# A two-layer graph network over 64 graphs: intermediate sums and scores in PSUM, byte masks, a third transposition tile, and new instruction orders

## The chip, the cores and the metric

The kernel runs on one core of one Trainium2 chip. Its engines work in parallel, each through its own queue in order: TensorE (PE) multiplies matrices into PSUM, which has eight banks of 128 partitions by 512 words of fp32; VectorE (DVE) and ScalarE (ACT) read and write PSUM and SBUF; GpSimd (POOL) works in SBUF alone; SyncE (SP) issues nearly all transfers here. PEld is TensorE's loading of weights. The metric is the device time of the whole program in microseconds (us).

## The reference

Input are 64 graphs of 256 nodes with 256 features each (`x`), with an adjacency `adj` of zeros and ones, and weights. Everything is fp32. Two layers follow each other; cut to what is computed:

```python
# layer 0
def gat(h, W, a):
    Wh = h @ W
    e = leaky_relu(Wh @ a[:F] + swap(Wh @ a[F:]), 0.2)
    att = softmax(where(adj > 0, e, -9e15), axis=1)
    return att @ Wh
h = layernorm(x + gat(gat(x, W1, a1), W2, a2)) * g + b          # norm A
x = layernorm(h + relu(h @ w_ff1 + b_ff1) @ w_ff2 + b_ff2)      # norm B, with g, b
# layer 1: 8 heads of 32
attn = softmax(q @ k.T / sqrt(32))
out = sum over r of (attn * (adj == r)) @ v_r                   # only r = 0 and 1 occur
x = layernorm(x + out @ Wo + bo)                                # norm C, with g, b
x = layernorm(x + gelu(x @ W1 + b1) @ W2 + b2)                  # norm D, with g, b
```

## The kernel before

A graph is small: 256 nodes are two tiles of 128 partitions, and the 256 features two blocks. Weights stay in SBUF. Most products over two by two blocks are made with seven instead of eight block products (`seven_products`: pieces `a` to `e` on TensorE, `k1` to `k4` that take a block out of PSUM, `p1` to `p3` that add to it).

One graph's work is cut into 194 **pieces**, each a function that issues a few instructions, named stage.piece. Each engine runs its instructions in the order in which the pieces are called, and nothing reorders them. Three lists set that order. `PERIOD` is one turn of the steady loop: an entry `G.gA0/0` calls piece `gA0` of stage G for the graph that is 0 behind the newest, `T.fd/5` a piece for the graph five behind. So six graphs are in flight. `START` and `END` are written-out lists for the first and last turns; setup pieces (S) stand in START. TensorE's steps in one turn, in the order of the list before: wh0, T.hd, wh1, ve, f1, eA, T.he, sc0, o0, o1, F.ha, F.hb, wo, F.hc, T.fa, T.fb, F.hd, gA0, gA1, T.fc, va, vb, eB, T.fd, F.he, vc, T.fe, q, k, T.ha, gB, T.hb, sc1, vd, T.hc, f0.

The pieces that the text speaks of:

- **L**: `xT`, `adj`, `x` load a graph. `joint_weights` (L338) makes the product `w12` of W1 and W2 and the four extra columns of `wx` once, ahead of the first graph.
- **G**, the two graph attentions (function `gat`, L732). `away` turns the adjacency into bytes that are 1 where there is no edge (L739) and takes its maximum (L742). `wh0`, `wh1` project; `wc` copies out. For step A: `eA` transposes one column into PSUM (L763), `lrA` on ACT writes the scores `s` to SBUF (L771), `adA` on DVE applies the leaky slope (L776), adds the mask (L777) and takes the maximum (L779), `exA` on ACT takes exponentials in place (L784), `rzA` divides the projected rows by their sums into `whz` (L791, L794), `gA0`, `gA1` multiply (L800), `wd` copies out. Step B is the same with `eB` to `rzB`, and ends in `gB`, tile `gat_b`.
- **Norms** (L493): `ln` adds the residual to the product in PSUM and writes `acc` in SBUF (L502), then takes statistics (L507 to L510); `rs` on POOL makes the factor (L514); `nm` normalises on DVE into `y` (L519). `ra`, `rb` on POOL scale and shift for the next residual.
- **Transpositions** (`turned`, L461): `dt` transposes 16-bit pairs by DMA into `pairs` (L469), `dm` moves halves by two transfers into `halves` (L477), and `c` (or `mg` for a head) joins them by a copy (L484), on ACT but for two heads that go to POOL. All these transfers are issued on SP in order. Eleven transpositions a graph share the tiles `pairs` and `halves`.
- **F**, the first feed-forward: `s` sums on POOL, `ha` to `he` with `hk`, `hp`, then `r` (ReLU), `f0`, `f1`; then `q`, `k` with their evictions `qe`, `ke`.
- **A**, the heads, two groups of four: `sc` scores, `mx` maxima (DVE), `ex` exponentials (ACT), `rz`, `sp` scaling (POOL), `dt`, `dm`, `mg` transposition, `pm` the mask (DVE, L922: the head's weights times the adjacency), `va` to `ve` the values, `o` outputs, `oc` evictions.
- **T**: `wo`, norm C, the second feed-forward (`ha` to `he`, GELU in `ge`, sums `u` on POOL, `fa` to `fe` with keeps `fk` on DVE at L713 and sums `fp`), norm D, `out`.

All PSUM tiles come from one tag of eight buffers, one bank each (`mm_tile`, L208).

Of the kernel before, what the change touches and what calls it, by code (L numbers as in the profile page):

```python
# [1312 lines left out]
```

## Time and profile before

| What | Value |
|---|---|
| Time, median of 3 runs | 3129.46 us (3119.91 to 3135.92) |
| The profiled execution: time, span | 3121.47 us, 3119.7 us |
| Mean granted TensorE clock | 0.992 |
| DMA moved | 449.41 MB, 144 GB/s |
| Heads' mask, L922 | 512 times, mean 1123 ns |
| Heads' transposition | 1024 transfers of halves (two for each of 512), 3.3 us to landing |

The page is of one profiled execution. A group's line gives the source line, engine, operation, output and inputs with shapes, count, then busy us, mean ns of one, and the engine's idle time just before it with what ended it. A busy PE includes the overlap of pipelined products, so its share says less than the spacing of like products does.

### The profile page before, as it was taken

How to read it: one execution, taken by the hardware profiler on the slowest of the kernel's cores; microseconds unless marked ns; L12 is line 12 of the kernel's file. 1: busy time of each engine (PE TensorE's matmuls, PEld its weight loads, DVE VectorE, ACT ScalarE, POOL GpSimd, SP SyncE). 2: the span in 40 equal slices, each digit the busy share in tenths (PEclk: the TensorE clock that was granted, in tenths of full speed). 3: DMA queues.
4: the chain of work that ended last, by engine and by line, in shares of the span. 5: the costliest groups of instructions: out<-in, count | busy, mean ns of one | idle time of the engine just before them, and what ended most of it. 6: DMA issues, size and time to landing. Idle time of an engine off the chain costs nothing.

```text
span 3119.7 us, 68789 instructions
## 1 busy us (share of the span) xinstructions
PE 3007.0 (96%) x23270; PEld 2629.7 (84%) x23270; DVE 2747.0 (88%) x5744; ACT 2548.7 (82%) x5822; POOL 2290.2 (73%) x3057
## 2 busy tenths in 40 slices
PE   6899999999999999999999999999999999999986
PEld 5788888888888888888898888888888888888876
DVE  5689999899998899898999899999999999889965
ACT  2688888888888888888888888888888888878874
POOL 4568777777777777777777777777777777777765
PEclk9999999999999999999999999999999999999998
DMA  5577766677676777776676666677677776767663
GB/s 156 108 145 149 149 149 143 146 155 143 149 151 137 142 146 151 148 152 138 155 150 144 148 142 145 150 152 147 147 153 145 149 149 143 146 138 151 149 133 73
DMA packets 1023941, 449.41 MB, mean 144 GB/s; under 512 B 771008, under 2 KB 1021888, under 8 KB 1023584
## 3 DMA queue, kind: packets, MB, share of 16 engines
q1 hardware_dynamic: 1022320, 442.70, 67.9%
q8 instruction: 188, 3.08, 0.5%
q0 software_dynamic: 976, 1.72, 0.4%
q14 instruction: 169, 1.38, 0.2%
q10 hardware_dynamic: 288, 0.52, 0.1%
HBM read 58.87 MB, written 16.78 MB: 24 GB/s over the span
## 4 chain that ended last, share of the span: by engine, by line
PE 68%; DVE 12%; DMA 8%; issue 3%; ACT 3%; POOL 1%; SPq 1%; DVEq 0%; ACTq 0%; POOLq 0%
PE ff_a L686 11%; PE hX_c L661 6%; PE o L930 5%; PE fX_c L702 5%; PE hX_a L661 4%; PE sc L880 3%; PE q L835 3%; PE hY_c L661 3%; PE k L835 3%; PE gat_b L800 3%; PE vX L848 3%; PE wh L747 3%; DVE pm L922 2%; PE wo L949 2%; DMA adj<-in_adjT 2%
## 5 line engine op out<-in xcount | busy, mean ns | idle before, releaser
L484 ACT COPY pm<-halves_p 128x1024 uint16<-128x1024 uint16 x384 | 522.4, 1360 | 137.8 <-DMA halves_p<-pairs_p 135.7
L922 DVE TENSOR_TENSOR pm<-pm,adj 128x512 f32<-128x512 f32 x512 | 565.6, 1123 | 19.3 <-POOL pm L484 12.2
L686 PE MATMUL ff_a<-w_L_gnn_w_ff,hid_a 128*128 128x256 f32 x2048 | 463.0, 379 | 0.1
L686 PEld LDWEIGHTS ff_a<-w_L_gnn_w_ff,hid_a 128*128 128x128 f32 x2048 | 384.0, 190 | 50.4 <-ACT hid_a L678 0.8
L484 POOL COPY pm<-halves_p 128x1024 uint16<-128x1024 uint16 x128 | 180.2, 1408 | 157.5 <-DMA halves_p<-pairs_p 140.4
L930 PE MATMUL o<-pm,v 128*32 128x256 f32 x4096 | 235.3, 381 | 5.5 <-POOL p L907 2.4
L678 ACT ACTIVATE hid_a<-hid_a,col_L_gnn_b_ff 128x256 f32<-128x256 f32 x512 | 230.1, 500 | 3.3 <-DVE hid_a L637 3.2
L678 ACT ACTIVATE hid_c<-hid_c,col_L_gnn_b 128x256 f32<-128x256 f32 x512 | 224.4, 498 | 5.1 <-DVE hid_c L637 2.4
L930 PEld LDWEIGHTS o<-pm,v 128*32 128x32 f32 x4096 | 126.2, 110 | 104.6 <-issue 15.9
L702 PE MATMUL fX_c<-f_L_gnn_W,hid_c 128*128 128x128 f32 x1536 | 207.2, 278 | 7.3 <-ACT hid_c L678 5.1
L514 POOL TENSOR_TENSOR rstd_a<-var_a,neghalf 128x2 f32<-128x2 f32 x64 | 45.0, 702 | 222.5 <-DVE var_a L510 222.5
L702 PEld LDWEIGHTS fX_c<-f_L_gnn_W,hid_c 128*128 128x128 f32 x1536 | 192.8, 192 | 13.2 <-ACT hid_c L678 5.8
L661 PEld LDWEIGHTS hX_a<-cols_a,f_L_gnn_w_ff 128*128 128x128 f32 x1024 | 126.9, 195 | 33.1 <-ACT hid_c L678 22.2
L880 PE MATMUL sc<-kT,qT 32*128 32x256 f32 x2048 | 149.6, 400 | 3.3 <-ACT p L894 2.8
L584 POOL TENSOR_TENSOR S_c<-cols_c 128x128 f32<-128x128 f32 x128 | 58.3, 455 | 128.4 <-ACT cols_c L484 128.4
L800 PE MATMUL gat_a<-whz_A,s_A 128*128 128x258 f32 x512 | 134.9, 400 | 18.2 <-DVE whz_A L794 15.4
L661 PE MATMUL hX_a<-cols_a,f_L_gnn_w_ff 128*128 128x128 f32 x1024 | 144.6, 285 | 6.4 <-ACT cols_a L484 5.0
L747 PE MATMUL wh<-wx,xT 128*128 128x260 f32 x512 | 136.0, 390 | 12.5 <-DVE wx L372 10.1
L661 PEld LDWEIGHTS hX_c<-S_c,f_L_gnn_W 128*128 128x128 f32 x1024 | 134.0, 191 | 8.5 <-ACT hid_c L672 1.3
L702 PE MATMUL fY_c<-f_L_gnn_W,H_c 128*128 128x128 f32 x1024 | 137.3, 278 | 3.8 <-POOL H_c L584 3.8
L661 PE MATMUL hX_c<-cols_c,f_L_gnn_W 128*128 128x128 f32 x1024 | 135.8, 276 | 2.7 <-ACT cols_c L484 2.7
L661 PE MATMUL hX_a<-S_a,f_L_gnn_w_ff 128*128 128x128 f32 x1024 | 136.9, 277 | 0.0
(2760 smaller groups left out, 9808.9 us busy)
## 6 DMA issues: line engine op xcount, KB each, us to landing
halves_p<-pairs_p SPq DMA_DIRECT2D x1024, 128.0 KB, 3.3
xT<-in_xT SPq DMA_DIRECT2D x64, 256.0 KB, 3.4
adj<-in_adjT SPq DMA_DIRECT2D x64, 256.0 KB, 3.5
x<-in_x SPq DMA_DIRECT2D x64, 256.0 KB, 3.5
halves_y_a<-pairs_y_a SPq DMA_DIRECT2D x128, 128.0 KB, 3.0
halves_y_y<-pairs_y_y SPq DMA_DIRECT2D x128, 128.0 KB, 3.5
halves_y_c<-pairs_y_c SPq DMA_DIRECT2D x128, 128.0 KB, 3.2
out<-res_d SPq DMA_DIRECT2D x64, 256.0 KB, 2.6
```

What stands on the lines that cost most here:

```text
L484: copy(into().bitcast(U16).rearrange("p (n s) -> p s n", s=2), t["halves"].rearrange("p s k q -> p s (k q)"),)
L661: nc.tensor.matmul(ps[:, f * P : (f + 1) * P], weights()[0][:, factor, f * P : (f + 1) * P], left, start=start and f == 0, stop=f == FC // ...
L678: nc.scalar.activation(tiles["hid"][:, f, :], tiles["hid"][:, f, :], func, bias=b1[:, f : f + 1])
L686: nc.tensor.matmul(tiles["ff"][:, i, :], tiles["hid"][:, f, nodes(i)], weights()[2][:, f, :], start=(f == 0), stop=(f == FC - 1),)
L702: nc.tensor.matmul(ps, left[:, f, :], weights()[2][:, factor, f * P : (f + 1) * P], start=start and f == 0, stop=f == FC // 2 - 1, skip_gr ...
L747: nc.tensor.matmul(t["whp", j], tiles["xT"][:, c, nodes(j)], wx[:, c, :], start=(c == 0), stop=(c == KC - 1),)
L800: nc.tensor.matmul(ps, t["s"][:, j, nodes(i)], t["whz"][:, j, :width], start=(j == 0), stop=(j == NT - 1),)
L835: nc.tensor.matmul(t[key + "p"][:, o, :], w[:, c, nodes(o)], tiles["cols"][:, c, :], start=(c == 0), stop=(c == KC - 1),)
L848: nc.tensor.matmul(ps, left, wv[:, factor, :], start=start, stop=True, skip_group_check=True)
L880: nc.tensor.matmul(t["sc", g, hh][:, i, :], qkv["q"][hd, g, nodes(i)], qkv["k"][hd, g, :], start=True, stop=True,)
L922: nc.vector.tensor_tensor(pm[:, 1, :], pm[:, 0, :], tiles["adj"], ALU.mult)
L930: nc.tensor.matmul(ps[hh * DH : (hh + 1) * DH, :], qkv["v"][:, j, d0 : d0 + DH], t["pm", (g, hh)][:, r, j * N : (j + 1) * N], start=(r == ...
```

## The change

- **Norms A, B and C:** the sum is written back into the product's PSUM tile; statistics and `nm` read it there, and the tile is let go after `nm`. The `acc` tiles in SBUF serve only norm D and setup.
- **First attention:** `e` takes a whole bank. The slope step reads `s` in SBUF and writes `e`, the mask step and the maximum work in `e`, and the exponentials read `e` and write `s`. One `s` tile instead of two.
- **Heads' mask:** `pm` compares the bytes of `away` with 0 and multiplies, instead of multiplying by the 32-bit adjacency. `away` has four tiles instead of one, `adj` one instead of four.
- **Tiles:** three each of `pairs`, `halves` and `S` instead of two.
- **Joint weights:** W1 is loaded on ACT's queue, its column products stand ahead of those of the joint product, and sums are written straight into `wx`.
- **Orders:** PERIOD, START and END are new. PERIOD has the same 194 pieces; 25 of them have another lag. TensorE's steps now: f0, T.hd, f1, wh0, T.he, wh1, sc0, o0, o1, T.fa, wo, eA, T.fb, F.ha, F.hb, T.fc, F.hc, va, T.fd, gA0, F.hd, gA1, T.fe, vb, F.he, eB, k, q, vc, T.ha, sc1, T.hb, vd, gB, ve, T.hc.

```diff
@@ -41,120 +41,121 @@
 PERIOD = """
-G.nmA/1 A.mx13/3 A.rz12/3 F.raB/4 F.sB/3 T.hk3/5 A.mx11/3 A.rz10/3 L.xT/0 T.hp3/5 A.vp2/4 A.dm02/4
-A.pm03/4 G.wh0/0 A.mg02/4 T.hd/5 A.ex13/3 T.hp2/5 G.wh1/0 A.ex11/3 A.sp12/3 A.dm00/4 G.wc0/0
-A.sp10/3 G.wc1/0 A.ve/4 A.pm01/4 F.dtA/1 A.mg00/4 F.dmA/1 F.f1/2 A.pm02/4 G.eA/0 A.pm00/4 T.rbC/5
-F.rbB/4 A.vk4/4 T.he/5 T.ge0/5 A.rz11/3 A.pm11/4 A.rz13/3 A.dt10/3 F.lnB/2 A.sc0/3 A.o0/4 T.ge1/5
-A.mx00/3 G.lrA/0 F.cA/1 T.hk4/5 A.o1/4 T.ge2/5 A.sp11/3 A.sp13/3 A.mx02/3 A.dt12/3 F.ha/1 A.oc0/4
-T.ge3/5 L.adj/0 A.oc1/4 F.sA/1 A.ex00/3 F.hb/1 A.mx03/3 G.away/0 A.dm10/3 A.dm12/3 F.rsB/2 F.hk1/1
-F.hk2/1 T.wo/4 A.mx01/3 G.adA/0 A.mg10/3 T.u0/5 F.hp1/1 T.lnC/4 F.hc/1 T.u1/5 A.mg12/3 A.dt13/3
-G.exA/0 F.raA/1 A.dt11/3 F.nmB/2 A.ex03/3 A.dm13/3 G.rzA/0 T.fa/5 F.hk3/1 A.ex02/3 T.rsC/4 T.fb/5
-F.hd/1 T.nmC/4 G.gA0/0 T.u3/5 T.fk1/5 T.fk2/5 A.rz03/3 A.ex01/3 T.u2/5 F.hp2/1 L.x/0 F.hp3/1
-A.mg13/3 A.sp03/3 G.gA1/0 A.pm12/3 G.wd0/0 G.wd1/0 A.dm11/3 A.rz01/3 T.fc/5 A.va/3 A.vb/3 F.dtB/2
-T.fk3/5 A.mg11/3 F.rbA/1 A.sp01/3 F.r0/1 A.pm13/3 T.dtC/4 A.rz02/3 A.vk1/3 G.eB/0 T.fd/5 F.dmB/2
-T.fp1/5 A.vk2/3 G.lrB/0 T.fp2/5 F.cB/2 F.he/1 A.vc/3 T.dmC/4 T.fe/5 A.rz00/3 F.r1/1 G.adB/0
-A.dt03/3 T.cC/4 A.dt01/3 F.q/2 A.vk3/3 G.exB/0 F.hk4/1 A.vp3/3 T.fp3/5 F.qe0/2 F.k/2 A.sp02/3
-T.fk4/5 F.r2/1 T.ha/4 F.qe1/2 A.dm03/3 F.ke0/2 T.hk1/4 T.lnD/5 G.rzB/0 T.nmD/5 A.sp00/3 T.sC/4
-G.gB/0 A.vp1/3 T.hb/4 A.dm01/3 T.rsD/5 A.dt02/3 T.raC/4 F.ke1/2 T.rbD/5 T.hp1/4 A.sc1/2 T.out/5
-A.dt00/3 G.lnA/0 A.mg03/3 T.hk2/4 F.r3/1 A.mg01/3 A.mx12/2 A.mx10/2 A.vd/3 G.rsA/0 T.hc/4 A.pm10/3
-F.f0/1 A.ex12/2 A.ex10/2
+T.hk3/5 A.ex12/3 F.f0/2 A.mx10/3 T.hd/5 A.pm00/4 G.rsA/1 A.vk4/4 L.xT/0 A.mg02/4 A.dm03/4 T.hp3/5
+F.f1/2 T.raC/5 A.ex10/3 G.nmA/1 T.hp2/5 A.pm02/4 A.mg03/4 A.rz12/3 G.wh0/0 T.he/5 T.ge0/5 L.adj/0
+A.pm01/4 T.ge1/5 G.wc0/0 A.sp13/3 A.dt11/3 F.dtA/1 A.pm03/4 T.rbC/5 F.lnB/2 A.sp12/3 A.dm11/3
+T.hk4/5 A.dt13/3 A.pm12/4 A.rz10/3 G.wh1/0 T.ge2/5 A.sc0/3 F.rsB/2 A.mx02/3 A.o0/4 F.dmA/1 T.ge3/5
+G.wc1/0 F.nmB/2 A.sp10/3 F.raA/1 A.o1/4 A.mx03/3 T.u0/5 A.mx01/3 T.fa/5 A.dt12/3 A.mx00/3 A.ex02/3
+A.dm13/3 L.x/0 A.oc0/4 A.oc1/4 F.cA/1 F.dtB/2 T.wo/4 A.dt10/3 G.away/0 G.eA/0 T.u1/5 T.u3/5
+A.ex03/3 A.ex01/3 G.lrA/0 F.sA/1 T.fk1/5 F.dmB/2 T.fp1/5 T.fb/5 A.mg11/3 F.ha/1 A.dm10/3 T.lnC/4
+F.hb/1 T.fk2/5 G.adA/0 A.rz03/3 A.rz01/3 T.fc/5 T.rsC/4 T.u2/5 F.hk1/1 F.hk2/1 A.sp01/3 T.nmC/4
+F.hc/1 T.fk3/5 F.hp1/1 A.ex00/3 G.exA/0 F.hk3/1 A.va/3 T.dtC/4 A.mg13/3 A.rz02/3 F.cB/2 G.rzA/0
+T.fp3/5 A.pm11/3 F.hp3/1 T.fd/5 A.sp02/3 G.gA0/0 F.hd/1 G.wd0/0 F.raB/3 T.fp2/5 A.mg10/3 A.rz00/3
+G.gA1/0 A.sp00/3 F.hp2/1 A.vk1/3 T.fe/5 T.fk4/5 A.vb/3 A.vk2/3 G.wd1/0 T.lnD/5 A.pm13/3 F.r0/1
+F.he/1 A.dt01/3 G.eB/0 F.k/2 F.q/2 A.vp1/3 F.r1/1 T.dmC/4 G.lrB/0 T.cC/4 A.dm12/3 G.adB/0 F.ke0/2
+F.hk4/1 F.ke1/2 A.vc/3 A.vk3/3 A.sp03/3 T.sC/4 A.dm01/3 T.ha/4 F.qe0/2 F.qe1/2 G.exB/0 A.dt00/3
+A.dt02/3 T.hk1/4 A.vp3/3 A.sc1/2 T.hb/4 A.vd/3 T.nmD/5 G.rzB/0 F.r2/1 T.hp1/4 A.mx11/2 A.mg01/3
+A.mx13/2 A.dt03/3 T.rsD/5 F.rbB/3 A.dm00/3 G.gB/0 T.hk2/4 A.vp2/3 A.pm10/3 T.rbD/5 A.mx12/2 F.r3/1
+A.ex11/2 F.rbA/1 A.mg12/3 A.rz11/2 A.dm02/3 G.lnA/0 A.ex13/2 F.sB/2 A.mg00/3 T.out/5 A.rz13/2
+A.ve/3 A.sp11/2 T.hc/4
 """.split()
...
@@ -322,7 +323,7 @@
             nc.sync.dma_start(out=tiles["xT"], in_=xT[b].rearrange("(c p) n -> p c n", p=P))
 
         def adjacency():
-            adj = tiles["adj"] = io.tile([P, NT * N], I32, tag="adj", name=f"adj_{b}", bufs=4)
+            adj = tiles["adj"] = io.tile([P, NT * N], I32, tag="adj", name=f"adj_{b}", bufs=1)
             nc.sync.dma_start(
                 out=adj.rearrange("p (t i) -> p t i", t=NT),
                 in_=adjT[b].rearrange("(t p) i -> p t i", p=P),
@@ -343,13 +344,15 @@
             work.tile([P, KC, D], F32, tag="y", name=f"in_{n}", bufs=3) for n in ("w1T", "w2", "w1")
         )
         a1, a2 = (work.tile([P, 2, D], F32, tag="acc", name=f"in_{n}", bufs=2) for n in ("a1", "a2"))
-        for a, n in ((a2, "L0_gnn_a2"), (a1, "L0_gnn_a1")):
+        for a, n in ((a1, "L0_gnn_a1"), (a2, "L0_gnn_a2")):
             nc.scalar.dma_start(
                 out=a.rearrange("p s d -> p (s d)"),
                 in_=t[n].rearrange("n one -> (n one)").partition_broadcast(P),
             )
-        for w, n in ((w1T, "L0_gnn_W1T"), (w2, "L0_gnn_W2"), (w1, "L0_gnn_W1")):
-            nc.sync.dma_start(out=w, in_=t[n].rearrange("(c p) n -> p c n", p=P))
+        for queue, w, n in (
+            (nc.sync, w1T, "L0_gnn_W1T"), (nc.scalar, w1, "L0_gnn_W1"), (nc.sync, w2, "L0_gnn_W2"),
+        ):
+            queue.dma_start(out=w, in_=t[n].rearrange("(c p) n -> p c n", p=P))
         for entry in ("L.xT", "L.adj", "L.x"):
             first.pop(entry)()
         ps = mm_tile("w12")
@@ -359,17 +362,14 @@
                     ps[:, o, :], w1T[:, c, nodes(o)], w2[:, c, :],
                     start=(c == 0), stop=(c == KC - 1),
                 )
-        nc.vector.tensor_copy(wx[:, :, :D], ps)
-        for w, a, at in ((wx, a2, SRC2), (w1, a1, SRC1)):
+        for w, a, at in ((w1, a1, SRC1), (wx, a2, SRC2)):
+            if w is wx:
+                nc.vector.tensor_copy(wx[:, :, :D], ps)
             for c in range(KC):
-                both = small.tile([P, 2], F32, tag="wa", name=f"wa_{at}_{c}", bufs=1)
                 prod = work.tile([P, 2, D], F32, tag="res", name=f"prod_{at}_{c}", bufs=3)
-                nc.vector.tensor_tensor(
-                    prod, a, w[:, c, :D].unsqueeze(1).to_broadcast([P, 2, D]), ALU.mult
-                )
-                nc.vector.tensor_reduce(both, prod, AX.X, ALU.add)
-                nc.vector.tensor_copy(wx[:, c, at : at + 1], both[:, 1:2])
-                nc.vector.tensor_copy(wx[:, c, at + 1 : at + 2], both[:, 0:1])
+                for half in range(2):
+                    nc.vector.tensor_tensor(prod[:, half, :], a[:, 1 - half, :], w[:, c, :D], ALU.mult)
+                nc.vector.tensor_reduce(wx[:, c, at : at + 2], prod, AX.X, ALU.add)
         return wx
 
 
@@ -465,14 +465,14 @@
         t = {}
 
         def turn():
-            t["pairs"] = work.tile([P, 2, 4, P], U16, tag="pairs", name=f"pairs_{name}", bufs=2)
+            t["pairs"] = work.tile([P, 2, 4, P], U16, tag="pairs", name=f"pairs_{name}", bufs=3)
             nc.sync.dma_start_transpose(
                 out=t["pairs"].rearrange("p c k q -> p (c k) q"),
                 in_=src().rearrange("p c a b n -> p (c a b n)").bitcast(U16),
             )
 
         def part():
-            t["halves"] = work.tile([P, 2, 4, P], U16, tag="halves", name=f"halves_{name}", bufs=2)
+            t["halves"] = work.tile([P, 2, 4, P], U16, tag="halves", name=f"halves_{name}", bufs=3)
             for c in range(2):
                 nc.sync.dma_start(
                     out=t["halves"][c * 64 : (c + 1) * 64].rearrange("p s k q -> p s (k q)"),
@@ -493,13 +493,13 @@
     def layernorm(do, stage, key, name, src, last=None):
 
 
+
         tiles = {}
 
         def sums():
-            acc, *terms = src()
-            if terms:
-                acc = work.tile([P, NT, D], F32, tag="acc", name=f"acc_{name}", bufs=2)
-                nc.vector.tensor_tensor(acc, *terms, ALU.add)
+            acc, *residual = src()
+            if residual:
+                nc.vector.tensor_tensor(acc, acc, *residual, ALU.add)
             tiles["acc"] = acc
             stats = small.tile([P, NT, 6], F32, tag="stats", name=f"stats_{name}", bufs=2)
             mv = tiles["mv"] = small.tile([P, NT, 2], F32, tag="mv", name=f"mv_{name}")
@@ -587,7 +587,7 @@
 
 
         def sums():
-            s = tiles["S"] = work.tile([P, 4, P], F32, tag="S", name=f"S_{name}", bufs=2)
+            s = tiles["S"] = work.tile([P, 4, P], F32, tag="S", name=f"S_{name}", bufs=3)
             cols = tiles["cols"]
             blocks = [cols[:, c, nodes(i)] for i in range(NT) for c in range(KC)]
             add_sums(nc.gpsimd, blocks, [s[:, n, :] for n in range(4)], range(4))
@@ -735,9 +735,9 @@
         t = {}
 
         def away():
-            t["away"] = work.tile([P, NT, N], U8, tag="away", name=f"away_{b}", bufs=1)
+            tiles["away"] = work.tile([P, NT * N], U8, tag="away", name=f"away_{b}", bufs=4)
             nc.vector.tensor_scalar(
-                t["away"].rearrange("p t i -> p (t i)"), tiles["adj"], 0.0, 1.0, ALU.is_le, ALU.mult
+                tiles["away"], tiles["adj"], 0.0, 1.0, ALU.is_le, ALU.mult
             )
             nc.vector.tensor_reduce(most[:, b : b + 1], tiles["adj"].bitcast(U32), AX.X, ALU.max)
 
@@ -758,31 +758,34 @@
 
         def targets(step, col):
 
-            ps = t["e"] = mm_tile(f"e_{step}{b}", (P, N))
+            t["e"] = mm_tile(f"e_{step}{b}", (P, NT, N))
             for i in range(NT):
                 nc.tensor.transpose(
-                    ps[:, nodes(i)],
+                    t["e"][:, 0, nodes(i)],
                     t["wh", step][:, i, col : col + 1].to_broadcast([P, P]), ident,
                 )
 
         def terms(step, col):
-            s = t["s"] = work.tile([P, NT, N], F32, tag="s", name=f"s_{step}{b}", bufs=2)
+            s = t["s"] = work.tile([P, NT, N], F32, tag="s", name=f"s_{step}{b}", bufs=1)
             for j in range(NT):
                 nc.scalar.activation(
-                    s[:, j, :], t["e"], AF.Identity, bias=t["wh", step][:, j, col : col + 1]
+                    s[:, j, :], t["e"][:, 0, :], AF.Identity,
+                    bias=t["wh", step][:, j, col : col + 1],
                 )
 
         def maximum(step):
-            nc.vector.scalar_tensor_tensor(t["s"], t["s"], ALPHA, t["s"], ALU.mult, ALU.max)
-            nc.vector.scalar_tensor_tensor(t["s"], t["away"], NEG, t["s"], ALU.mult, ALU.add)
+
+            nc.vector.scalar_tensor_tensor(t["e"], t["s"], ALPHA, t["s"], ALU.mult, ALU.max)
+            away = tiles["away"].rearrange("p (t i) -> p t i", t=NT)
+            nc.vector.scalar_tensor_tensor(t["e"], away, NEG, t["e"], ALU.mult, ALU.add)
             t["m"] = small.tile([P, NT], F32, tag="gm", name=f"gm_{step}{b}")
-            nc.vector.tensor_reduce(t["m"], t["s"], AX.X, ALU.max, negate=True)
+            nc.vector.tensor_reduce(t["m"], t["e"], AX.X, ALU.max, negate=True)
 
         def exps(step):
             t["z"] = small.tile([P, NT], F32, tag="gz", name=f"gz_{step}{b}")
             for j in range(NT):
                 nc.scalar.activation(
-                    t["s"][:, j, :], t["s"][:, j, :], AF.Exp,
+                    t["s"][:, j, :], t["e"][:, j, :], AF.Exp,
                     bias=t["m"][:, j : j + 1], accum_out=t["z"][:, j : j + 1],
                 )
 
@@ -821,7 +824,7 @@
             do[f"G.ad{step}"], do[f"G.ex{step}"] = partial(maximum, step), partial(exps, step)
             do[f"G.rz{step}"] = partial(over_sums, step, width)
         do["G.gB"] = second
-        return layernorm(do, "G", "A", f"a{b}", lambda: (None, t["gat"], tiles["x"]))
+        return layernorm(do, "G", "A", f"a{b}", lambda: (t["gat"], tiles["x"]))
 
     def projections(do, b, tiles):
 
@@ -919,7 +922,9 @@
         def by_relation(h):
 
             pm = t["pm", h]
-            nc.vector.tensor_tensor(pm[:, 1, :], pm[:, 0, :], tiles["adj"], ALU.mult)
+            nc.vector.scalar_tensor_tensor(
+                pm[:, 1, :], tiles["away"], 0.0, pm[:, 0, :], ALU.is_equal, ALU.mult
+            )
 
         def outputs(g):
             ps = t["op", g] = mm_tile(f"o_{b}_{g}", (P, N))
@@ -974,12 +979,12 @@
         scaled(do, "F", "A", f"a{b}", a, "L0_gnn_g_ln1", "L0_gnn_b_ln1")
         combine(do, "F", "A", f"a{b}", a)
         feed_forward(do, "F", f"a{b}", a, lambda: ff0, "r", AF.Relu, seven=False)
-        y = layernorm(do, "F", "B", f"b{b}", lambda: (None, a["ff"], a["res"]))
+        y = layernorm(do, "F", "B", f"b{b}", lambda: (a["ff"], a["res"]))
         to_columns(do, "F", "B", f"y{b}", y, "ACT")
         scaled(do, "F", "B", f"b{b}", y, "L0_gnn_g_ln2", "L0_gnn_b_ln2")
         combine(do, "F", "B", f"y{b}", y)
         heads = attention(do, b, projections(do, b, y), tiles)
-        c = layernorm(do, "T", "C", f"c{b}", lambda: (None, heads["wo"], y["res"]))
+        c = layernorm(do, "T", "C", f"c{b}", lambda: (heads["wo"], y["res"]))
         to_columns(do, "T", "C", f"c{b}", c, "ACT")
         scaled(do, "T", "C", f"c{b}", c, "L1_gnn_g1", "L1_gnn_beta1")
         combine(do, "T", "C", f"c{b}", c)
```

## The prediction

> **What bounds it now.** First the shares of busy time, then the stretches, then the waits.
>
> ```profile
> PE 3007.0 (96%) x23270; PEld 2629.7 (84%) x23270; DVE 2747.0 (88%) x5744; ACT 2548.7 (82%) x5822; POOL 2290.2 (73%) x3057
> ...
> PE 68%; DVE 12%; DMA 8%; issue 3%; ACT 3%; POOL 1%; SPq 1%; DVEq 0%; ACTq 0%; POOLq 0%
> ```
>
> TensorE is the bound, but 12% of the chain that ended last is VectorE and 8% DMA. The next view gives busy us of each engine in a stretch: the start, the end, and two stretches of the steady part.
>
> ```profile
> 0.00:78.00 78.00, 50.93 (x215) 41.86 (x216) 41.85 (x90) 21.02 (x55) 35.77 (x51) 0.91 0.60 156
> 1404.00:1482.00 78.00, 74.98 (x597) 64.52 (x597) 69.27 (x138) 64.19 (x149) 59.58 (x77) 1.00 0.67 138
> 1482.00:1560.00 78.00, 78.00 (x622) 68.53 (x624) 72.48 (x156) 67.49 (x152) 60.33 (x85) 1.00 0.69 155
> 3042.00:3120.00 78.00, 53.92 (x400) 47.36 (x398) 43.17 (x101) 33.81 (x62) 42.87 (x50) 0.87 0.31 72
> ```
>
> In the steady part PE is full or nearly so, and VectorE (third) is at 89 to 93%. Pace: the first product of `gat_b` comes once per graph. From the fifth (181 us) to the last (2942 us) its spacing is 46.8 us on average and 45.7 at its smallest, which I take as PE's own work. So 1.1 us x 59 = 65 us are stalls in the steady part; that is the prize. The waits view, of PE alone and then of the others, names them (engine, line, waited-for: us in total, times, longest):
>
> ```profile
> PE gat_a L800 <- DVE whz_A L794: 15.4, 25, 2.7
> PE fX_c L702 <- DVE acc_c L713: 12.0, 34, 1.1
> PE q L835 <- ACT cols_y L484: 9.1, 13, 1.4
> PE fZ_c L702 <- DVE hid_a L637: 4.5, 5, 1.7
> ...
> DVE away L739 <- DMA adj<-in_adjT: 64.3, 44, 3.6
> ACT cols_y L484 <- DMA halves_y_y<-pairs_y_y: 59.5, 62, 2.3
> ACT cols_c L484 <- DMA halves_y_c<-pairs_y_c: 22.5, 21, 9.6
> ...
> SPq L469 <- DMA halves_p<-pairs_p: 370.6, 335, 3.5
> ```
>
> Counted instead as the excess of each PE start over its usual spacing (216 ns for 256 columns, 112 for 128), the same four places lose 22, 21, 12 and 7 us: 62 of the 65. Three of them wait for VectorE, the fourth for a join copy.
>
> **The change, part by part.** Per graph, against the 46.8.
>
> *Norms from PSUM.* The sum costs the same: it reads one PSUM operand already (L502, 665 to 688 ns). The normalising pair (L519) now reads PSUM. Groups: busy us, mean ns, idle before.
>
> ```profile
> L519 DVE TENSOR_SCALAR y_c<-acc_c,mv_c,rstd_c 128x256 f32<-128x256 f32 x128 | 106.8, 873 | 2.9 <-POOL rstd_c L514 2.7
> ...
> L777 DVE SCALAR_TENSOR_TENSOR s_A<-away,s_A 128x512 f32<-128x512 uint8 x64 | 90.9, 1421 | 2.2
> ...
> L519 DVE TENSOR_SCALAR y_b<-acc_b,mv_b,rstd_b 128x256 f32<-128x256 f32 x128 | 52.5, 451 | 2.1 <-POOL rstd_b L514 1.8 <-issue 0.3
> ...
> L637 DVE TENSOR_TENSOR v<-v,vX 128x256 f32<-128x256 f32 x64 | 26.0, 407 | 1.6 <-PE vX L848 1.6
> ```
>
> Here a rule speaks against the change. The Trainium skill, "VectorE: DVE Perf Modes", "Rules for kernel authors", tells one who does many operations on a product to copy it out of PSUM first, since a PSUM source loses the double rate; its errata section has 58 + n/2 cycles from SBUF against 120 + n from PSUM, at 0.96 GHz 194 against 392 ns for 256 columns: six would cost 1.2 us more. The rows differ: `y` from SBUF never took under 398 ns, so no double rate is seen, and it takes up to 1555, while operations with one PSUM operand (`v`, 256 columns) stay between 400 and 423. I go by the rows: 6 at 0.41, saving 2 x (873 + 697 + 451 - 3 x 410) = 1.6 us. Bounds: +1.2 to -1.6. The statistics read PSUM too: no such row; 411 ns taken, as for a product of that width.
>
> *Scores in PSUM.* The mask step (L777) loses one of two SBUF operands: (1421 + 837) - 2 x 690 = 0.9 us saved. The same skill's "SBUF — State Buffer", section "SBUF: two separate sides", has a VectorE operation with two SBUF inputs and a GpSimd one exclude each other; the spread 679 to 1797 ns of L777 beside 671 to 689 of the one-operand L779 agrees. No VectorE write into PSUM is in the trace: between 0.66 (as a read) and the 1.42 of now; I take 0.69. The first step (L776) still reads `s` twice: unchanged. The exponentials read PSUM, as the heads' do (520 to 540 ns against 497 and 511): +0.1 us on ScalarE.
>
> *Heads masked by bytes.* Still two SBUF operands of 512; the byte row's minimum is 679 against 660: +0.15 us for eight, else the 1123 of today.
>
> VectorE's saving: 1.6 + 0.9 - 0.15 = 2.3 us.
>
> *Order: adjacency.* Today VectorE waits 1.0 us a graph for `adj`, because `L.adj` stands 0.9 us of PE work ahead of `G.away`. In the new list it is 9.1 us, against 3.5 us to landing. One `adj` tile is enough: its two readers are done 36 us before the next load. -1.0 us on VectorE.
>
> *Three pairs and halves.* A transpose (L469) waits on SP for the halves' transfer that still reads its pair tile: 370.6 us for heads, and every other transfer stands behind it in SP's queue. The third tile takes most of that away. The new list uses it: between `dmB` and `cB` 8.1 us of PE work instead of 0, at the heads' joins on ScalarE mostly 4 to 10 instead of 1 to 4.5. So the 59.5 us of `cols_y` and the stall at `q` should mostly go.
>
> *PE's order.* The same products in other places; what counts is PE work between a result and its PE user, in list order. `fc` to `fd` (needs VectorE's keep, L713): 1.5 before (va, vb, eB), 2.6 after (hc, va). `f1` to the first of q and k: 24.2 to 25.1. `gB` to `ha`: 20.0 to 22.1. Shorter: `eA` to `gA0` 15.4 to 8.9; q to `sc1` 4.5 to 2.6 (two evictions of 0.47 each); `o1` to `wo` 2.6 to 1.8 (one of 0.47); `gA1` to `eB` 3.1 to 2.2 (one of 0.37).
>
> The first is the one to work out. Today `whz_A` ends 15.6 us after `eA`: VectorE starts the chain only 6.7 us after `eA`, and reaches the reciprocal 2.2 us after the exponentials. The work itself is 0.9 + 3 x 0.69 + 1.1 + 0.15 + 0.7 to 1.7 = 5 to 6 us. In the new queues VectorE has two keeps, the norm C sum (2.2) and one keep ahead: maximum from 3 to 5.1. ScalarE has then a join (1.36), two evictions (1.2) and one head's exponentials (1.25) ahead of `exA`: to about 7.1; `whz_A` 8.0 to 9.0, against 8.9. The B chain today does the same in 7.3 of 8.8 and PE waited there once. So about even, some 0.1 us of stall instead of 0.37.
>
> *PSUM held longer.* Scores, `gat_b` and `wo` keep a bank 4 to 5 us longer, but `f0` and `f1` now adjoin and `vX`, `hX` are let go sooner: by list order the 8 banks are held 220 us of PE work a graph against 216, of 363. No cost taken; +0.2 us if one reuse turns late.
>
> *Start.* PE waits 10.1 us for `wx`. W1's products now run while W2 loads, and four column copies go; behind `w12` stay a copy (0.69), four products of 256 (0.41) and two sums (0.69), 3.7 us. But W2 now stands behind xT and adj on SP. From 22.0 to about 18.5: -3 us (0 to -7). *End:* new order, PE idle there 35 us in 156; taken as 0, bounds +-10.
>
> **Sum.** Of the 50 us of stalls behind VectorE I take two thirds off (3.3 us more slack a graph), of q's 12 half: -39. The shortened places give back 6 (0.1 us a graph). Start -3. Together -36 on the profiled 3121.5: 3085. That run lies 8 below the median of those shown (3129.5), inside their 3120 to 3136; I say 3087. All stalls gone, start and end at their best: 3121 - 65 - 7 - 10 = 3039.
>
> **Rivals.**
> 1. *The slack buys nothing* (0.16). PE is full already and only start and tail remain: 3110 to 3125. For it: 96% busy. Against: 62 us of stalls with a named releaser, three of four VectorE.
> 2. *A late join holds ScalarE's queue* (0.17), slower. In the new list `T.cC` stands directly behind `dmC`, with no PE work between, and ahead of k's and q's evictions and `exB`; who waits is `sc1` and `gB`. The halves need 3.2 us; today this join waits 22.5 us in all, once 9.6. `dmC` stands on SP behind a head's transpose that waits for GpSimd. Margin: `nmC` stands at 24.3 us of PE work in the list; 0.8 for itself, 3.4 for the transpose and 3.2 for the halves make 31.7, and ScalarE reaches the join 0.9 after `eB`'s end at 32.9. So 2.1 us; beyond them each us costs 59. From 0.6 us past the margin (36 / 59) it eats the gain; at 1.2 the time is 3085 + 71 = 3156. Against: GpSimd is 73% busy, and the third tile clears the queue before it.
> 3. *VectorE gains less* (part of the main case's range): PSUM operands as the rule has them, +1.2 instead of -1.6. Then only `adj` and the order help, half the gain: 3103.
>
> **Chances.** Main case with rival 3: 0.67, 3045 to 3110. Measurements of this kernel can't tell under 0.5% (16 us) from none. Two thirds of rival 1 fall within it; rival 2 is slower by over 0.5% nearly always. Faster 0.73, same 0.11, slower 0.16. Range 3043 to 3140, which leaves out the better half of rival 2's harm and the very best.
>
> **What would show it.** `y_a`, `y_b`, `y_c` near 410 ns each with little spread; the mask step near 690; `away`'s and `cols_y`'s waits nearly gone; SP's waits at L469 a fraction of 517 us (four rows); spacing of `gat_b` near 46.1. Wrong: mean `y` over 600; a wait of ScalarE on `halves_y_c` over 100 us; PE waiting for ScalarE at `sc` or `gat_b`; spacing at 46.8 or more.

## The result, and the profile after

The changed kernel takes 3080.8 us (median of 4 runs, 3079.4 to 3082.0), the one before on the same chip 3127.8: ratio 0.985, 95% interval 0.982 to 0.988. The forecast was 3087.

The page of the changed kernel, shares of busy time and the chain that ended last; then its stretches, as shown of before.

```profile
PE 2986.0 (97%) x23270; PEld 2612.6 (85%) x23270; DVE 2541.0 (83%) x5740; ACT 2556.1 (83%) x5822; POOL 2176.1 (71%) x3057
...
PE 84%; DVE 11%; DMA 2%; issue 1%; ACT 1%; POOL 0%; SPq 0%; DVEq 0%; POOLq 0%; ACTq 0%
```

```profile
1404.00:1482.00 78.00, 76.89 (x585) 68.82 (x585) 66.80 (x155) 67.19 (x154) 54.63 (x80) 1.00 0.71 145
1482.00:1560.00 78.00, 77.43 (x627) 67.96 (x626) 64.95 (x149) 65.92 (x149) 55.23 (x79) 1.00 0.84 150
```

DMA has left the chain (8% to 2%), and VectorE has shed 206 us. Yet PE isn't full in the steady stretches, where it was in one of them before. By the starts of `gat_b` (fifth, last, end of span), the 40 us come from three places:

| | fifth `gat_b` | 59 turns of | last to end | span |
|---|---|---|---|---|
| before | 181.4 | 46.78 | 178.1 | 3119.7 |
| after | 171.7 | 46.49 | 164.9 | 3079.8 |
| gain, us | 9.7 | 17.1 | 13.2 | 39.9 |

The waits of the changed kernel: PE's, then the others', then SP's (what waited, for what: us in all, times, longest).

```profile
PE gat_b L803 <- DVE hid_c L637: 33.1, 59, 0.6
...
PE gat_a L803 <- DVE whz_A L797: 5.1, 2, 4.9
PE k L838 <- ACT cols_y L484: 3.9, 4, 1.5
```

```profile
ACT pm L484 <- DMA halves_p<-pairs_p: 41.9, 57, 2.1
...
ACT cols_c L484 <- DMA halves_y_c<-pairs_y_c: 15.0, 4, 11.3
...
ACT cols_y L484 <- DMA halves_y_y<-pairs_y_y: 5.0, 3, 2.3
```

```profile
SPq L469 <- DMA halves_p<-pairs_p: 109.4, 145, 2.7
...
SPq L469 <- DMA halves_y_y<-pairs_y_y: 22.3, 26, 1.3
...
SPq L469 <- DMA halves_y_c<-pairs_y_c: 7.0, 13, 1.0
```

The four old stalls are gone: `gat_a` waits twice instead of 25 times, `fX_c` hardly, and VectorE's wait for `adj` (64.3) no longer appears. Of SP's four rows at L469, 517 us before, three are left, with 139. But one wait is new: `gat_b` waits in each of the 59 turns for `hid_c`, which isn't its input. The order of time around it, in the changed kernel (start, us, then what ran; in brackets the idle time before):

```profile
1515.50 2.82 DVE L529 SCALAR_TENSOR_TENSOR res_d<-acc_c,mv_d,row_L_gnn_g 128x256 f32<-128x256 f32 x2
...
1518.24 0.15 DVE L794 RECIPROCAL grz_B<-gz_B 128x2 f32<-128x2 f32 x1
1518.42 0.90 DVE L797 TENSOR_SCALAR whz_B<-wh_B,grz_B 128x256 f32<-128x256 f32 x2
...
1519.24 0.67 DVE L637 TENSOR_TENSOR hid_c<-hid_c,hZ_c 128x512 f32<-128x512 f32 x1
...
1519.97 1.78 PE L803 MATMUL gat_b<-whz_B,s_B 128*128 128x256 f32 x7 [0.57 <-DVE hid_c L637]
```

`whz_B` is ready at 1519.3, but PE starts only at 1519.97, just after VectorE has added `hZ_c` (`T.hp1`, until 1519.91). I read this as a wait for the PSUM tile: `gat_b` takes the one that held `hZ_c`, which is free once its last reader is done, and that reader stands behind norm D's `nm` (2.8 us) and `rzB`. VectorE's own groups, and at the end one of before:

```profile
L925 DVE SCALAR_TENSOR_TENSOR pm<-away,pm 128x512 f32<-128x512 uint8 x512 | 408.2, 808 | 3.7 <-ACT pm L484 2.5 <-POOL pm L484 1.2
L529 DVE SCALAR_TENSOR_TENSOR res_d<-acc_c,mv_d,row_L_gnn_g 128x256 f32<-128x256 f32 x128 | 170.9, 1373 | 0.0
...
L519 DVE TENSOR_SCALAR y_a<-gat_b,mv_a,rstd_a 128x256 f32<-128x256 f32 x128 | 63.4, 537 | 1.8 <-POOL rstd_a L514 1.7
L519 DVE TENSOR_SCALAR y_b<-ff_a,mv_b,rstd_b 128x256 f32<-128x256 f32 x128 | 63.2, 536 | 1.9 <-POOL rstd_b L514 1.9
L519 DVE TENSOR_SCALAR y_c<-wo,mv_c,rstd_c 128x256 f32<-128x256 f32 x128 | 62.5, 530 | 1.9 <-POOL rstd_c L514 1.9
...
L780 DVE SCALAR_TENSOR_TENSOR e_A<-away,e_A 128x512 f32<-128x512 uint8 x64 | 44.5, 696 | 2.2
```

```profile
L529 DVE SCALAR_TENSOR_TENSOR res_d<-acc_c,mv_d,row_L_gnn_g 128x256 f32<-128x256 f32 x128 | 62.4, 526 | 0.0
```

The `y` steps cost 0.53, not 0.41 us. The heads' mask `pm`, which I had at 1123 to 1142 ns, fell to 808, and norm D's `res_d` rose from 526 to 1373.

### The profile page after: what moved, and what is told of

It reads as the page before. It is cut to its first block, busy times and chain, and to the rows that moved or that the text cites. A ratio compares the mean times of both kernels' runs of the same rounds, so it can differ in the third digit from the quotient of the medians.

```text
span 3079.8 us, 68797 instructions
## 1 busy us (share of the span) xinstructions
PE 2986.0 (97%) x23270; PEld 2612.6 (85%) x23270; DVE 2541.0 (83%) x5740; ACT 2556.1 (83%) x5822; POOL 2176.1 (71%) x3057
## 3 DMA queue, kind: packets, MB, share of 16 engines
q0 software_dynamic: 976, 1.72, 0.3%
## 4 chain that ended last, share of the span: by engine, by line
PE 84%; DVE 11%; DMA 2%; issue 1%; ACT 1%; POOL 0%; SPq 0%; DVEq 0%; POOLq 0%; ACTq 0%
PE ff_a L686 14%; PE fX_c L702 7%; PE hX_a L661 7%; PE o L935 7%; PE hX_c L661 5%; DVE res_d L529 5%; PE gat_b L803 4%; PE gat_a L803 4%; PE k L838 4%; PE hY_a L661 4%; PE q L838 4%; PE wh L747 4%; PE fY_c L702 4%; PE wo L954 3%; PE vX L851 3%; PE sc L883 2%
## 5 line engine op out<-in xcount | busy, mean ns | idle before, releaser
L925 DVE SCALAR_TENSOR_TENSOR pm<-away,pm 128x512 f32<-128x512 uint8 x512 | 408.2, 808 | 3.7 <-ACT pm L484 2.5
L484 POOL COPY pm<-halves_p 128x1024 uint16<-128x1024 uint16 x128 | 172.3, 1346 | 11.1 <-DMA halves_p<-pairs_p 11.0
L529 DVE SCALAR_TENSOR_TENSOR res_d<-acc_c,mv_d,row_L_gnn_g 128x256 f32<-128x256 f32 x128 | 170.9, 1373 | 0.0
L803 PE MATMUL gat_b<-whz_B,s_B 128*128 128x256 f32 x512 | 127.3, 391 | 36.3 <-DVE hid_c L637 33.1
L803 PEld LDWEIGHTS gat_b<-whz_B,s_B 128*128 128x128 f32 x512 | 91.7, 189 | 71.0 <-DVE hid_c L637 56.8
L661 PEld LDWEIGHTS hX_c<-cols_c,f_L_gnn_W 128*128 128x128 f32 x1024 | 134.0, 192 | 17.6 <-ACT cols_c L484 8.3
L661 PEld LDWEIGHTS hY_c<-S_c,f_L_gnn_W 128*128 128x128 f32 x1024 | 125.9, 193 | 19.9 <-issue 19.6
L661 PE MATMUL hY_c<-S_c,f_L_gnn_W 128*128 128x128 f32 x1024 | 142.6, 283 | 0.0
L672 ACT COPY hid_c<-hX_c 128x512 f32<-128x512 f32 x192 | 113.3, 590 | 34.0 <-PE hX_c L661 30.4
```

The costliest lines, as they stand in the source:

```text
L484: copy(into().bitcast(U16).rearrange("p (n s) -> p s n", s=2), t["halves"].rearrange("p s k q -> p s (k q)"),)
L529: nc.vector.scalar_tensor_tensor(tiles["res"][:, i, :], tiles["acc"][:, i, :], tiles["mv"][:, i, 0:1], rows[last[0]], ALU.subtract, ALU.mult,)
L661: nc.tensor.matmul(ps[:, f * P : (f + 1) * P], weights()[0][:, factor, f * P : (f + 1) * P], left, start=start and f == 0, stop=f == FC // ...
L803: nc.tensor.matmul(ps, t["s"][:, j, nodes(i)], t["whz"][:, j, :width], start=(j == 0), stop=(j == NT - 1),)
L925: nc.vector.scalar_tensor_tensor(pm[:, 1, :], tiles["away"], 0.0, pm[:, 0, :], ALU.is_equal, ALU.mult)
```

## The experiments

Theory: VectorE's work is shorter (fewer operands in SBUF), and that is what the stalls behind VectorE yielded to. Rivals: the third tile of pairs did it, through SP's queue; the new orders did it; and PSUM tiles held longer take some of it back. Each ratio is against the kernel before on the same chip. Spacings and times by tile below are worked out from the traces: from the start of a PE product to the start of the next, credited to the tile of the later one (so that the wait ahead of a product is its own), mean of 50 graphs, in us.

**1. One part alone, old lists.** `old_norms`:

```diff
-            acc, *terms = src()
-            if terms:
-                acc = work.tile([P, NT, D], F32, tag="acc", name=f"acc_{name}", bufs=2)
-                nc.vector.tensor_tensor(acc, *terms, ALU.add)
+            acc, *residual = src()
+            if residual:
+                nc.vector.tensor_tensor(acc, acc, *residual, ALU.add)
```

> The kernel before with one part alone: the sums of the norms A, B and C are written into the PSUM tile of their product; the lists of steps are the old ones. All theories expect y_a, y_b and y_c near 535 ns each, against 697 / 451 / 873 (0.8 us of VectorE a graph less). Theory 'VectorE's time itself was the gain': 0.8 of the 2.3 us that I had put on shorter VectorE work shows at once in the stalls behind VectorE, about 8 to 15 us: 3112 to 3119. Rival 'the order was the gain': the waits for adj (64 us) and at SP (370 us) stay and the place of the work in the queues decides, so nothing is gained: 3123 to 3133. Rival 'the banks held longer cost': 3135 or more, with PE waiting for a norm.

Measured: 1.007 (1.004 to 1.010), 3158 us. Two rows of VectorE's groups, then from the view of the tile `ff_a` what PE's idle time in front of it ended with (us, times):

```profile
L793 DVE TENSOR_SCALAR whz_A<-wh_A,grz_A 128x258 f32<-128x258 f32 x128 | 143.2, 1159 | 2.3
...
L518 DVE TENSOR_SCALAR y_c<-wo,mv_c,rstd_c 128x256 f32<-128x256 f32 x128 | 63.0, 531 | 1.9 <-POOL rstd_c L513 1.7
```

```profile
its engine sat idle before it (us, times) until:
  ACT p L893: 20.7, 66
```

`y` is cheaper, as in the full change, and `whz_A` dearer (842 to 1159); VectorE is busy 2704.5 us instead of 2747.0. `gat_a` and `fX_c` take 0.18 and 0.30 us less a graph, by the shorter steps or by the slower turn (`pairs3_norms` below shows no such gain). But `ff_a` takes 0.4 us more, `wo` and `fY_c` 0.3 each. `ff_a` now waits for the heads' exponentials, which aren't its input: a bank again, by the same reading (before, `ff_a` waited 0.1 us in all). Net it is 0.6 us a graph longer, as the third theory above had it.

`old_bytes` (byte mask, `away` four tiles, `adj` three):

```diff
-            nc.vector.tensor_tensor(pm[:, 1, :], pm[:, 0, :], tiles["adj"], ALU.mult)
+            nc.vector.scalar_tensor_tensor(
+                pm[:, 1, :], tiles["away"], 0.0, pm[:, 0, :], ALU.is_equal, ALU.mult
+            )
```

> The kernel before with one part alone: the heads are masked from the bytes of away (is_equal, then times) and no longer from the 32-bit adj; the lists of steps are the old ones; adj has 3 tiles instead of 4 and away 4 instead of 1, which the memory needs. Theory 'the place beside GpSimd's work decides': pm of the mask step stays at a mean of 1100 ns or more (1123 before) and the time stays, 3120 to 3133. Rival 'the byte operand is what made it 808 ns': mean near 810, 2.5 us of VectorE a graph less, time 3095 to 3115.

Measured: 1.000 (0.998 to 1.002), 3134 us.

```profile
L924 DVE SCALAR_TENSOR_TENSOR pm<-away,pm 128x512 f32<-128x512 uint8 x512 | 570.5, 1132 | 24.6 <-POOL pm L484 14.9 <-ACT pm L484 9.6
```

So the byte operand is not what made `pm` 808 ns: in the old lists it stays at 1132 (and at 1114 with the third tile, below). That leaves its place in the new lists.

**2. The third tile alone.** `old_bytes_pairs3` and its control `old_bytes_adj2` (both with bytes, `adj` at two tiles, old lists) differ in one number:

```diff
-            t["pairs"] = work.tile([P, 2, 4, P], U16, tag="pairs", name=f"pairs_{name}", bufs=2)
+            t["pairs"] = work.tile([P, 2, 4, P], U16, tag="pairs", name=f"pairs_{name}", bufs=3)
```

> The kernel before with the bytes as in old_bytes (which left the time at 3134) and a third tile of pairs; halves stay at two, adj is at two, which the memory needs; the lists of steps are the old ones. Theory 'SP's queue, held by the pair tile, costs TensorE': the waits at L469 fall from some 517 us to under 200, ScalarE's wait for cols_y from 60 to under 15, and the 11 us that TensorE loses at q with it: 3118 to 3126. Rival 'the transfers were hidden': the waits on SP fall, TensorE's pace stays at 46.8 to 47.0, 3129 to 3138.

> The control of old_bytes_pairs3: the same kernel (old lists, bytes, adj at two tiles) with the two tiles of pairs of before. Theory 'the third tile of pairs is what gained 70 to 80 us': pace 46.8 to 47.1, 0.2% around the time of before. Rival 'two tiles of adj instead of four or three gained it (another time of loading)': 0.975 to 0.985 of before.

Measured: 0.978 (0.975 to 0.980), 3053 us, 65 us under what even the theory expected; the control 1.000 (0.998 to 1.002). One more tile of pairs gains more than the whole change. First three waits of the control, then the kernel with the third tile: the share of each engine, and waits of PE, of the others and of SP:

```profile
PE gat_a L802 <- DVE whz_A L796: 13.6, 19, 2.6
...
DVE away L739 <- DMA adj<-in_adjT: 53.8, 41, 3.4
...
SPq L469 <- DMA halves_p<-pairs_p: 367.3, 329, 3.6
```

```profile
PE 2978.8 (98%) x23270; PEld 2629.0 (86%) x23270; DVE 2723.5 (89%) x5744; ACT 2544.5 (83%) x5822; POOL 2294.7 (75%) x3057
```

```profile
PE gat_a L802 <- DVE whz_A L796: 2.6, 1, 2.6
...
ACT cols_y L484 <- DMA halves_y_y<-pairs_y_y: 35.2, 60, 2.2
...
DVE away L739 <- DMA adj<-in_adjT: 6.6, 2, 3.4
```

```profile
SPq L469 <- DMA halves_p<-pairs_p: 0.9, 2, 0.7
```

VectorE is as busy as before (2724 us against 2748 of the control), and PE hardly waits for it any more. (ScalarE's wait for `cols_y` fell to 35.2, not under 15.) So what had made VectorE late was not its work. The rows point to its wait for `adj`, which stood in SP's queue behind transposes waiting for a pair tile. The next run was to test that.

**3. Is it `adj`?** `old_adj_scalar_queue`: before, with one load on another queue.

```diff
-            nc.sync.dma_start(
+            nc.scalar.dma_start(
                 out=adj.rearrange("p (t i) -> p t i", t=NT),
```

> The kernel before with one edit: adj is loaded through ScalarE's queue instead of SP's, so that it no longer stands behind transposes that wait for their pair tile. The heads' transposes and halves stay as they were. Theory 'the stalls of gat_a and of keep (fX_c) behind VectorE are VectorE's wait for adj': that wait (64 us) goes, gat_a falls from 2.04 towards 1.65 and fX_c from 4.16 towards 3.8 us a graph, q keeps its 1.85: 0.984 to 0.990 of before. Rival 'they come from the halves of the heads as well': gat_a and fX_c keep half or more of their excess, 0.993 to 1.0.

Measured: 1.037 (1.035 to 1.039), 3242 us, so neither. VectorE waits more than three times as long for `adj`:

```profile
DVE away L739 <- DMA adj<-in_adjT: 215.4, 61, 8.9
...
ACT pm L484 <- DMA halves_p<-pairs_p: 157.0, 111, 3.9
```

Issue to landing is 3.5 us as before, but the load is issued late, as ScalarE's queue holds joins that wait for the same halves (157 us): from its issue to VectorE's arrival at `away` 0.2 us pass on average here, 3.0 before and 5.3 in `old_bytes_pairs3`. As a test of moving `adj` out of the way the run failed, but it gives a dose: with 151 us more of this wait, `gat_a`, `fX_c` and `fZ_c` took 0.69, 0.20 and 0.93 us more a graph, while `q` fell from 1.85 to 1.75. The trace of before shows the same turn by turn. In the 13 of 50 turns without a wait for `adj`, `gat_a`, `fX_c` and `fZ_c` took 1.68, 3.86 and 0.89 us, close to what they take with the third tile; in the 23 turns that waited 1 us or more, 2.45, 4.31 and 1.11; `q` took 1.85 in both. So the first three go with `adj`, and `q`, which needs `cols_y`, does not. These are times that move together: no run took away the wait for `adj` and left two pair tiles.

**4. Third tile and norms.** `pairs3_norms` is `old_bytes_pairs3` with the edit of `old_norms`.

> old_bytes_pairs3 with the sums of norms A, B and C in PSUM. Theory 'the norms in PSUM hold banks into the next user, whatever SP's queue does': ff_a, wo or fY_c are again 0.3 us longer each, the pace rises from 45.8 to 46.3 or more, 1.1 to 2% over old_bytes_pairs3 (ratio to before 0.987 to 0.998). Rival 'with the queue free VectorE reads the banks in time and its shorter norms help': ratio 0.974 to 0.980.

Measured: 0.997 (0.995 to 0.998), 1.9% over `old_bytes_pairs3`. `ff_a` +0.38, `wo` +0.32, `q` +0.28, `gat_a` +0.20: the bank cost is there with SP's queue free as well.

**5. Undone or moved in the new lists.** `new_scores_sbuf` keeps the scores in one `s` tile:

```diff
-            nc.vector.scalar_tensor_tensor(t["e"], t["s"], ALPHA, t["s"], ALU.mult, ALU.max)
+            nc.vector.scalar_tensor_tensor(t["s"], t["s"], ALPHA, t["s"], ALU.mult, ALU.max)
...
-            nc.vector.tensor_reduce(t["m"], t["e"], AX.X, ALU.max, negate=True)
+            nc.vector.tensor_reduce(t["m"], t["s"], AX.X, ALU.max, negate=True)
```

> The kernel after with one part undone: the first attention's scores stay in one SBUF tile (first step, mask, maximum and exponentials in SBUF; the PSUM tile of the products is let go after ScalarE's terms); the new lists of steps stay. Theory 'one operand less in SBUF matters': the mask step is at 850 to 1400 ns instead of 696, the chain to gat_a is longer by 0.5 to 1.5 us (slack 1.7 us) and the one to gat_b by as much (slack 0.65 us), so PE waits for whz_B: 3090 to 3130. Rival 'the new places keep it clear of GpSimd anyway': mask step under 800 ns, 3075 to 3087.

Measured: 0.980 (0.977 to 0.982), 3071 us, spacing 46.37 against 46.49 of the full change, though the mask step of chain A is long again:

```profile
L777 DVE SCALAR_TENSOR_TENSOR s_A<-away,s_A 128x512 f32<-128x512 uint8 x64 | 106.2, 1660 | 2.2
```

1 us more of VectorE work a graph in chain A cost PE nothing. The theory had the mask step's rise right (and too small); the time is below what either side forecast.

`nmD_late` (first) and `nmD_later` (second) move one step of PERIOD:

```diff
-A.dt02/3 T.hk1/4 A.vp3/3 A.sc1/2 T.hb/4 A.vd/3 T.nmD/5 G.rzB/0 F.r2/1 T.hp1/4 A.mx11/2 A.mg01/3
+A.dt02/3 T.hk1/4 A.vp3/3 A.sc1/2 T.hb/4 A.vd/3 G.rzB/0 F.r2/1 T.hp1/4 T.nmD/5 A.mx11/2 A.mg01/3
```

```diff
-A.dt02/3 T.hk1/4 A.vp3/3 A.sc1/2 T.hb/4 A.vd/3 T.nmD/5 G.rzB/0 F.r2/1 T.hp1/4 A.mx11/2 A.mg01/3
-A.mx13/2 A.dt03/3 T.rsD/5 F.rbB/3 A.dm00/3 G.gB/0 T.hk2/4 A.vp2/3 A.pm10/3 T.rbD/5 A.mx12/2 F.r3/1
+A.dt02/3 T.hk1/4 A.vp3/3 A.sc1/2 T.hb/4 A.vd/3 G.rzB/0 F.r2/1 T.hp1/4 A.mx11/2 A.mg01/3
+A.mx13/2 A.dt03/3 T.rsD/5 F.rbB/3 A.dm00/3 G.gB/0 T.hk2/4 A.vp2/3 T.nmD/5 A.pm10/3 T.rbD/5 A.mx12/2 F.r3/1
```

> The kernel after with one step of the repeated list moved: norm D's normalising step (T.nmD, two VectorE instructions of 1.4 us) goes from ahead of G.rzB to directly behind T.hp1; nothing else changes. Theory 'gat_b stalls because the bank that it takes is let go by T.hp1, which stands behind nmD': the regular stall of 0.6 to 0.8 us in front of gat_b goes, its spacing falls from 46.5 to 45.7 to 45.9, 59 times: 3032 to 3045. Rival 'gat_b is set by whz_B or another result, or the lost time turns up elsewhere': spacing stays above 46.3, 3070 to 3083.

> The kernel after with T.nmD moved further than in nmD_late: directly behind A.vp2 (whose end lets go the bank that the last vX product takes, where nmD_late lost 0.49 us a graph). Theory 'a bank let go behind nmD, once more': vX back to 1.53 us a graph, gat_b stays at 1.73, spacing 45.7, 59 times 0.49 less than nmD_late: 3030 to 3040. Rival 'each place of nmD delays something': a third place shows up, 3050 to 3066.

Measured: `nmD_late` 0.977 (0.974 to 0.979), 3062 us, spacing 46.15, between the two forecasts. The wait of `gat_b` is gone, and 0.49 of its 0.83 us came back one product later. The move brings `whz_B` earlier too, so that it was the bank rests on the order of time above, and on this one (VectorE, then PE), where `vX` waits for a step that makes none of its inputs:

```profile
1513.74 0.40 DVE L621 TENSOR_TENSOR v<-v,vX 128x256 f32<-128x256 f32 x1
```

```profile
1512.09 1.89 PE L787 MATMUL gat_b<-whz_B,s_B 128*128 128x256 f32 x8
1514.20 0.70 PE L835 MATMUL vX<-f_Wv,cols_y 128*128 128x256 f32 x2 [0.23 <-DVE v L621]
```

The next `vX` takes the tile that this `v` step lets go; the step now stands behind `nm`. `nmD_later` puts `nm` behind that step too: 0.972 (0.969 to 0.974), 3034 us, spacing 45.67 in every turn. By tile; old and new lists are to be read apart, since an interval has the length of the product ahead of it (216 ns for one of 256 columns, 112 for 128), and another neighbour shifts a cell by 0.1:

| | `gat_a` | `fX_c` | `q` | `ff_a` | `wo` | `gat_b` | `vX` | turn |
|---|---|---|---|---|---|---|---|---|
| before | 2.04 | 4.16 | 1.85 | 6.81 | 1.63 | 1.63 | 1.72 | 46.81 |
| `old_bytes_pairs3` | 1.66 | 3.78 | 1.70 | 6.81 | 1.63 | 1.63 | 1.72 | 45.77 |
| `pairs3_norms` | 1.85 | 3.77 | 1.98 | 7.18 | 1.94 | 1.63 | 1.72 | 46.93 |
| after | 1.54 | 4.08 | 1.73 | 6.70 | 1.63 | 2.56 | 1.53 | 46.50 |
| `nmD_late` | 1.54 | 4.08 | 1.73 | 6.70 | 1.63 | 1.73 | 2.02 | 46.16 |
| `nmD_later` | 1.54 | 4.08 | 1.73 | 6.70 | 1.63 | 1.73 | 1.53 | 45.67 |

A turn of 45.67 us is reached in the old lists as well: by 45 of the 59 turns of `old_bytes_pairs3`, and by 9 of before. Without stalls the new order of products is no quicker than the old.

`nmD_later_scores_sbuf` joins both edits:

> nmD_later with the first attention's scores in one SBUF tile, as in new_scores_sbuf. Theory 'the scores in SBUF gained only because res_d ran shorter (964 against 1373 ns) ahead of the late bank': with nmD out of the way nothing is left of that gain, the time is that of nmD_later within 4 us. Rival 'SBUF is the better place by itself': 6 to 10 us below nmD_later. Rival 'contention comes back': the mask step at 1.66 us in chain A, and 5 us or more above nmD_later.

Measured: 0.973 (0.971 to 0.976), 2.7 us over `nmD_later` on the same chip, with VectorE busy 2599.0 us instead of 2502.7. Nothing is left of what SBUF had gained (9 us by the spans), which fits that `res_d`, shorter there in `new_scores_sbuf` (964 against 1373 ns), stood ahead of the late bank. And 1.5 us more of VectorE work a graph costs next to nothing in these lists.

**6. The start.** `new_joint_old` and `nmD_later_joint_old` take back the loads and sums of `joint_weights` (three loads on SP, W2 second, four column copies):

```diff
-        for queue, w, n in (
-            (nc.sync, w1T, "L0_gnn_W1T"), (nc.scalar, w1, "L0_gnn_W1"), (nc.sync, w2, "L0_gnn_W2"),
-        ):
-            queue.dma_start(out=w, in_=t[n].rearrange("(c p) n -> p c n", p=P))
+        for w, n in ((w1T, "L0_gnn_W1T"), (w2, "L0_gnn_W2"), (w1, "L0_gnn_W1")):
+            nc.sync.dma_start(out=w, in_=t[n].rearrange("(c p) n -> p c n", p=P))
```

> The kernel after with the old preparation of the joint weights (all three loads on SP, W2 second, column copies); the rest stays. My sum had -3 us for the new one, the trace shows TensorE's first product for a graph 0.9 us earlier. Theory 'the start is set by the loads behind xT and adj': +1 us, 3080 to 3084. Rival 'the new preparation brought the 9 us that the fifth graph is earlier': 3087 to 3092.

> nmD_later with the old preparation of the joint weights, which took nothing away in new_joint_old (3078 against 3081 on another chip). Theory 'the two preparations are equal, since both wait for loads until 21 us': within 3 us of nmD_later, ratio 0.970 to 0.973. Rival 'the old one is better by its earlier start of the first products': ratio under 0.970.

Measured: 0.986 (0.983 to 0.988) and 0.970 (0.969 to 0.971), 3078 and 3032 us, against 0.985 and 0.972 with the new preparation, which so gains nothing; the first `wh` product starts at 21.3 us with the old one, at 21.1 with the new (22.0 before), though `w12` starts at 8.0 with the old one and at 14.8 with the new. `nmD_later_joint_old` is the fastest kernel run, 3.0% under before where the full change is 1.5% under. Against `old_bytes_pairs3` (3051.4), the span of `nmD_later` (3032.7) is 6.3 us shorter up to the fifth `gat_b`, 4.5 in the 59 turns and 7.9 from the last on: that is what the other parts and orders bring together once no bank is late.

## Why the prediction was right, and where it was not

The time was right by luck, as the errors of the terms cancelled, and the cause was wrong. Of the 36 us forecast, 33 were to come in the steady turns and 3 at the start; 17.1 came in the steady turns, 9.7 at the start and 13.2 at the end. What held was the prize: the 45.7 us a turn that I took for PE's own work is the pace of every turn of `nmD_later`.

- **The step that failed** is the first of the sum: "Of the 50 us of stalls behind VectorE I take two thirds off (3.3 us more slack a graph), of q's 12 half: -39". I read "waits for VectorE" as "VectorE has too much to do". The third tile alone takes off 1.0 us a graph, 59 of the 62 us counted, with VectorE's work all but unchanged; less work of VectorE (42 us in `old_norms`, 15 in `pairs3_norms`) came with longer turns, and 1.5 us more (`nmD_later_scores_sbuf`) cost 2.7 us in all. The profile had the chain: PE waits for VectorE, VectorE for `adj` (64.3), SP at L469 for halves (370.6). I used the second wait and the third, as small terms, and didn't join them to the first. That the second is the link between the other two is what the turns and the dose of section 3 support; it isn't isolated.
- **Adjacency, -1.0 us on VectorE:** the size was right. That `L.adj` must be moved for it was wrong; in `old_bytes_pairs3` it stands at its old place and the wait is 6.6.
- **PSUM held longer, "No cost taken; +0.2 us if one reuse turns late":** the mis-sized term. One reuse did turn late, at 0.83 us a graph (2.56 against 1.73 at `gat_b`), nearly as much as the third tile brings in the old lists (1.0); there the norms' part is 0.6 to 1.2. In the new lists the late tile is that of `hZ_c`, which the change doesn't hold longer: it is late by `nmD` and `rzB` ahead of its reader. Whether `gat_b` would find another tile free with the norms in SBUF isn't shown. The count of banks held (220 against 216) couldn't show it. What matters is what VectorE has queued ahead of the step that lets a tile go.
- **Norms:** 2 x (537 + 536 + 530) against 2 x 1230 ns was forecast: 0.75 us a graph too low; of the 1.6 us forecast 0.84 was saved. The rule's 392 ns and my row's 410 were both under the 535 measured. The spread is gone as I said (523 to 545), and the time doesn't notice either.
- **Scores:** mask step 696 ns, as forecast; worth nothing in time in the new lists. **Bytes:** +0.15 or nothing was right for the edit; the 2.5 us that `pm` lost come from its new place.
- **`eA` to `gA0`:** `whz_A` ends 7.0 us after `eA` (8 to 9 forecast), PE comes at 8.7: 8.9 was enough.
- **Start and end:** -3 and 0 were forecast, -9.7 (at the fifth `gat_b`) and -13.2 came. The joint weights' part was nothing. The third tile has 4.1 and 7.2 of it (control against `old_bytes_pairs3`); the new START and END have the rest only by subtraction.
- **Rivals.** 1 (only start and tail remain) is out as put, though 23 of the 40 us do come from there. 2 (late join `T.cC`): `cols_c` waited 4 times, 15.0 us in all, down from 22.5; out. 3 (PSUM operands dearer, +1.2 us instead of -1.6): the `y` rows came to -0.84, about a quarter of the way, and it didn't touch the time.

Left open: the new lists with two tiles of pairs, the old lists with the scores in PSUM, and the norms in SBUF in the new lists weren't tried. So whether shorter VectorE work alone, with no bank held longer, would have gained in the old lists isn't known.
